# A four-layer transformer stack on one core: layer 3's experts put ahead of its shared products for the first half of the tokens, and the last spreads and gathers paced by landings and memsets

## The chip, the core and the metric

The kernel runs on one core of a Trainium2 chip. Its engines work in parallel, each through its own list of instructions in order: TensorE (PE: matrix products and transposes; PEld is its weight load), VectorE (DVE), ScalarE (ACT), GpSimd (POOL) and SyncE (SP, which here only issues DMAs). POOL issues the DMAs whose rows are chosen by an index (DMA_INDIRECT in the profile). The metric is the device time of one execution in microseconds (us), lower is better. Three runs of the kernel before gave 1930.78, 1930.79 and 1932.56 us; the median is 1930.79 us.

## The reference

An activation x of 4 x 1024 tokens with 128 features passes through four layers; each is `x = layernorm(x + mix(x))`, then `x = layernorm(x + ffn(x))`. Only layer 3 and one list of layer 1 are touched here. Layer 3, cut to what matters:

```
# mix: gated Toeplitz unit; t = position, mixing runs over the batch index
xr = x / (rms(x) + 1e-8)
u, v = silu(xr @ u_w.T + u_b), silu(xr @ v_w.T + v_b)          # 256 features each
x = layernorm(x + (u * toeplitz(v)) @ o_w.T + o_b + x)
# ffn: 32 experts, 4 of them for each token, and one shared product of width 512
p = softmax(x @ router_w.T + router_bias)
top, idx = top_k(p, 4);  top = top / sum(top)
routed = sum_i top[i] * ( silu(x @ gate[idx[i]].T) * (x @ up[idx[i]].T) ) @ down[idx[i]].T
shared = ( silu(x @ sgate.T) * (x @ sup.T) ) @ sdown.T
x = layernorm(x + routed + shared)
```

Layer 1's ffn has the same form with 16 experts, 4 for each token. All is float32.

## The kernel before

**Tokens and parts.** x stays in SBUF as 32 tiles of 128 tokens. Layer 3 treats them in three parts: `a` is the first half (16 tiles), `b` and `c` are a quarter each (8 tiles). Layer 1's second half is the part `r` (16 tiles).

**One part's way through a routed ffn.** `l3_attn` mixes, `l3_route` picks experts and computes for each token and choice a row in a list sorted by expert (`positions`, which writes `posl3b` and the like). `spread` (line 1373 on) then writes the tokens into that list in DRAM, one indirect DMA for each tile and choice: 64 for `a` or `r`, 32 for `b` or `c`; each carries 128 rows of 512 bytes. `small_experts` (lists `l3ra`, `l3rb`, `l3rc` in, `l3ya`, `l3yb`, `l3yc` out) reads the list in groups of four tiles (`xg`), multiplies by the experts' weights on PE (`gu`, `tp`, `yp`) and writes the results back to DRAM by SP; there are 20 groups for `a` and 12 for `b` and for `c`. Further groups that only an uneven routing needs stand under a condition at the end (`rest_of`, line 1414), which each engine evaluates for itself; the name `made l3a` is noted there. `collect` (line 1441) gathers each token's four results, one indirect DMA each into a buffer `yt`, and DVE adds them with their weights into x (line 1452). `finish` norms and writes out. `l3_shared` makes the shared products (`pg`, `pu`, `hs`, `py`); for `a` it adds straight into x, for `b` and `c` into a buffer that is added later (`held`).

**What sets the order.** The program is emitted by Python generators. Each step that a generator yields has a cost in planned microseconds. `mix(main, side, pace, drain)` emits a step of `main` and then steps of `side` until their costs, times `pace`, are used up; a larger pace uses a side step's cost up faster. `abreast` emits the generator that is behind next. `when` holds a chain until a name has been noted. Each engine then works in the order that came out. `indirect` also forces the indirect DMAs to stay on POOL's queue in the order of emission.

**Pacing.** Under `spaced(gen, 1, 2, 1.45)` every indirect DMA waits, on POOL, until the one two places ahead of it has landed (`before`, line 1345), and the planner counts 1.45 us for it in place of 1.26. In the kernel before this holds for `r`'s spread and gathers in layer 1, for all of layer 2 but its last gathers, and for `a`'s spread in layer 3. The spreads of `b` and `c` and all gathers of layer 3 go without.

**The last stretch.** After layer 2's last experts (`l2_experts(n2)`), `on` holds what runs beside PE's main work: the last gathers of layer 2, mixing and routing of `b`, its spread, mixing and routing of `c`, the 64 gathers of `a` with the spread of `c` somewhere between, and the gathers of `b`. The main work is, in this order: shared products of `a`, experts of `a`, shared products of `b`, experts of `b`, shared products of `c`, experts of `c`. At last `close` gathers the 32 results of each choice and tile of `c`, norms and writes out.

Of the kernel before, what the change touches and what calls it, by code (L numbers as in the profile page):

```python
# [20 lines left out]
P = 128  # L21
# [21 lines left out]
E3, F3, K3 = 32, 128, 4  # L43
# [31 lines left out]
class Kernel:  # L75
    def __init__(self, ctx, tc, ins, out, cols, consts, rows):
        self.tc, self.nc, self.ins, self.out = tc, tc.nc, ins, out
        self.count = itertools.count()
        nc = self.nc
        self.const = self.pool(ctx, "const")  # L80
        self.small = self.pool(ctx, "small", 3)
        self.routes = self.pool(ctx, "routes")
        self.side = self.pool(ctx, "side", 2, space=PSUM)
        dram = self.pool(ctx, "dram", space=DRAM)

        self.cols_t = self.load(self.const, ins["cols"])
        self.cst_t = self.load(self.const, ins["consts"])
        self.x = self.tile(self.const, [P, NT, D], "x")
        self.xT = self.tile(self.const, [P, NT * P], "xT")
        nrow = ins["rows"].shape[1]  # L90
        self.rows_t = self.tile(self.const, [P, nrow], "rows")
        nc.gpsimd.dma_start(out=self.rows_t, in_=ins["rows"].to_broadcast([P, nrow]))
        self.col = {k: self.cols_t[:, a:b] for k, (a, b) in cols.items()}
        self.cst = {k: self.cst_t[:, a:b] for k, (a, b) in consts.items()}
        self.row = {k: self.rows_t[:, a:b] for k, (a, b) in rows.items()}
        self.ident = self.cst["ident"]
        self.eps = self.tile(self.const, [P, 1], "eps")
        nc.vector.memset(self.eps, LN_EPS)
        self.halfpi = self.tile(self.const, [P, 1], "halfpi")
        nc.vector.memset(self.halfpi, math.pi / 2)  # L100
        self.ones = self.tile(self.const, [P, E3], "ones")
        nc.vector.memset(self.ones, 1.0)
        self.rnd = self.tile(self.const, [P, 1], "rnd")
        nc.vector.memset(self.rnd, RND)
        self.drop = self.tile(self.const, [P, 1], "drop")
        nc.vector.memset(self.drop, -RND)
        self.zero = self.tile(self.const, [P, D], "zero")
        nc.gpsimd.memset(self.zero, 0.0)
        self.flag = self.tile(self.const, [1, 1], "flag", I32)
        self.hm = self.tile(self.const, [P, 4], "hmg")  # L110

        self.first, self.rest = Part("a", 0, 2), (Part("b", 2, 1), Part("c", 3, 1))
        self.parts = (self.first, *self.rest)
        self.by_rows = (
            Part("a", 0, 2, range(B), 0), Part("m", 2, 2, (0, 1), NT // 2), Part("n", 2, 2, (2, 3), 3 * NT // 4)
        )

        self.rows_done = 0

        self.listed = set()  # L120

        self.traced, self.latest = nc.cur_bb.bb.instructions, {}
        self.now = self.moved_by = 0.0
        self.moved = []
        self.landing = []
        self.spacing = None

        self.lists, self.route = {}, {}
        self.both = (self.first, Part("r", 2, 2))
        for lay, ne, k in (("l1", E1, K1), ("l2", E2, K2), ("l3", E3, K3)):  # L130
            for pt in {"l1": self.both, "l2": self.by_rows, "l3": self.parts}[lay]:
                tl = -(-((pt.nt * P * k + (P - 1) * ne) // P) // 4) * 4
                self.lists[lay, pt.name] = (
                    self.tile(dram, [tl * P, D], f"{lay}r{pt.name}"), self.tile(dram, [tl * P, D], f"{lay}y{pt.name}"), tl
                )
        self.wall2 = self.tile(dram, [P, E2 * 3 * F2], "wall2")
        self.xsave = self.tile(dram, [P, NT, D], "xsave")

        self.ksave = self.tile(dram, [P, B, BLK], "ksave")
        self.vsave = self.tile(dram, [P, B, 4, (NH + 1) * VW], "vsave")  # L140
# [769 lines left out]
    def l2_attn(self, hf):  # L910
# [6 lines left out]
        with ExitStack() as low, ExitStack() as ctx:  # L917
# [114 lines left out]

            last = 4 * hf + 3
            d0, d1, d3 = (last - 3, 512), (last - 2, 384), (last, 128)
            full = [(j, 512) for j in range(4 * hf)]
            alone = lambda m: [[(m, *p) for p in ps] for ps in ([d0], [d1, d3])]
# [336 lines left out]
    def spread(self, lay, part, k):  # L1373

        pos, _, _, done, _ = self.route[lay + part.name]
        rows = self.lists[lay, part.name][0]
        for t in range(part.nt):
            for i in range(k):
                ins = self.indirect(
                    apart=done,  # L1380
                    out=rows, out_offset=bass.IndirectOffsetOnAxis(ap=pos[:, t, i : i + 1], axis=0),
                    in_=self.x[:, part.order[t], :], in_offset=None,
                )
                done.append(ins)
            yield (self.step * k,)
        self.listed.add(lay + part.name)

# [501 lines left out]
    def at_once(self, gen):  # L1889

        for _ in gen:
            yield (0.0,)

    def served(self, gen, *others):

        others = list(others)
        while True:
            while others and others[0][0]():
                yield from others.pop(0)[1]
            got = next(gen, None)  # L1900
            if got is None and not others:
                return
            yield got or (1.0,)
# [35 lines left out]
        yield from self.l2_route(part)  # L1939
        yield from self.spread("l2", part, K2)  # L1940

    def last(self, part, yp):
        yield from self.collect("l3", part, K3, yp)
        yield from self.finish(part)

    def close(self, part, yp):
# [10 lines left out]
    def all(self):  # L1957
        a, rest = self.first, self.rest
        b, c = rest
        r = self.both[1]  # L1960
        a2, m2, n2 = self.by_rows
        with ExitStack() as ctx:
            lgp = self.pool(ctx, "l2lg")
            self.l2_lg = self.tile(lgp, [P, NT, E2], "lg")
            with ExitStack() as early:
# [14 lines left out]
                with ExitStack() as c2:  # L1980
                    wall = self.l1_wall(c2)
                    yp = self.pool(c2, "l1ya", 5, right=True)
# [3 lines left out]
            with ExitStack() as c2:  # L1986
# [3 lines left out]
                yp = self.pool(c2, "l1yr", 5, right=True)  # L1990
                self.run(self.mix(self.chain(self.l1_experts(r, wall), self.l1_shared(r)), self.chain(loads, self.spaced(self.routed(a2), 1, 2, 1.45))))
                self.run(self.mix(self.l2_experts(a2, wall2), self.spaced(self.l1_close(r, yp), 1, 2, 1.45)))
            listed = lambda name: lambda: name in self.listed
# [6 lines left out]
            with ExitStack() as c3:  # L2000
                with ExitStack() as c2:
                    wall = self.l2_wall(c2)
                    self.press(on, listed("l2m"))
                    self.run(self.mix(self.l2_experts(m2, wall), on, drain=False))
                    self.press(on, lambda: {"l2n", "routed l3a"} <= self.listed)
                    sw, wall3 = self.l3_wall(c3, True)
                    on = self.chain(on, self.spaced(self.rows_in(m2), 1, 2, 1.45))
                    self.run(self.mix(self.l2_experts(n2, wall), on, drain=False))
                self.press(on, listed("l3a"))
                yp = self.pool(c3, "l3y", 8)  # L2010

                on = self.chain(
                    on, self.collect("l2", n2, K2, yp, which=(0, 1, 4, 5)),
                    self.abreast(
                        self.chain(self.l3_attn(b), self.mark("mixed l3b"), self.l3_route(b)),
                        self.collect("l2", n2, K2, yp, which=(2, 3, 6, 7)),
                    ),
                    self.abreast(
                        self.chain(
                            self.spread("l3", b, K3), self.when(listed("made l3a")), self.last(a, yp),  # L2020
                        ),
                        self.chain(
                            self.l3_attn(c), self.mark("mixed l3c"), self.l3_route(c),
                            self.at_once(self.spread("l3", c, K3)),
                        ),
                    ),
                    self.when(listed("made l3b")), self.last(b, yp),
                )
                self.run(self.mix(self.chain(self.l3_shared(a, sw), self.l3_experts(a, wall3)), on, 0.45, False))
                hold = self.pool(c3, "l3hold", 2)  # L2030
                for p in (b, c):
                    self.press(on, listed("mixed l3" + p.name))
                    sh = self.tile(hold, [P, QT, D], "sh")
                    self.run(self.mix(self.l3_shared(p, sw, sh), on, 0.75, False))
                    self.press(on, listed("l3" + p.name))
                    self.press(on, listed("mixed l3c"))
                    ahead = self.chain(self.held(p, sh), on) if p is c else self.held(p, sh)
                    self.run(self.mix(self.l3_experts(p, wall3, ahead), on, 0.75, False))
                self.run(self.close(c, yp))
        bad = self.nc.values_load(self.flag[0:1, 0:1], min_val=0, max_val=1)  # L2040
        with self.tc.If(bad > 0):  # L2041
            with ExitStack() as ctx:
# [9 lines left out]
                for p in self.parts:  # L2052
                    self.run(self.onward(p))
                    with ExitStack() as c2:
                        sw, wall = self.l3_wall(c2)
# [167 lines left out]
```

## Time and profile before

| what | value |
|---|---|
| median of three runs | 1930.79 us |
| the profiled execution, its own time | 1937.33 us |
| its span, first to last instruction | 1935.5 us |
| mean granted TensorE clock | 0.896 of full |
| busy in the span: PE / DVE / ACT / POOL | 1541.5 / 1199.2 / 900.6 / 690.3 us |
| layer 3's experts of `a`, their gathers start on POOL | 1712.8 us into the span |
| last matmul of `c`'s experts ends | 1865.6 us |
| `c`'s 32 gathers start | 1877.6 us |
| last of them is issued | 1920.3 us |

Durations below come from the profiled execution, whose own time is 6.5 us (0.34%) above the median of the runs. A row of the timeline gives start, duration, engine, source line, operation, tile written and read, and in brackets the idle time of the engine before it and what ended that idle time ("issue" is time for which the profile shows no wait). The share of a whole engine says little here: what counts is which engine has work without a gap in the last 400 us.

### The profile page before, as it was taken

To read this page: it belongs to the slowest core of one execution; us is meant where nothing else is said; L and a number is where in the kernel's file an instruction comes from. 1 tells how busy PE (TensorE), PEld (TensorE's weight loads), DVE (VectorE), ACT (ScalarE), POOL (GpSimd) and SP (SyncE) were. 2 spreads that over 40 slices of the span, in tenths; PEclk is the share of its full clock that TensorE was granted. 3 is DMA by queue.
4 is the path that set the end of the run, shared out by engine and by line. 5 is a ranking of instruction groups with operands and counts; after the bars stand their busy time and mean duration, and the time that the engine had idled before them with its cause. 6 is when DMAs were issued, how large, how long until landed. Compare 5 with 4: busy or idle time off the path is not lost. (4 is left out here: it accounts for less than half of the span.)

```text
span 1935.5 us, 27095 instructions
## 1 busy us (share of the span) xinstructions
PE 1541.5 (80%) x9025; PEld 920.8 (48%) x9025; DVE 1199.2 (62%) x3491; ACT 900.6 (47%) x1349; POOL 690.3 (36%) x670
## 2 busy tenths in 40 slices
PE   7885677597847887989977878798798998999850
PEld 3332433385423345856632232333355757768650
DVE  8998698465766664635564565546442446866383
ACT  5876265243324554423336756564532236644330
POOL 2000148604630660265443000030536430567775
PEclk9897688798978998999988988898988999989985
DMA  9990002244430113632241000000452213425452
GB/s 297 288 288 10 1 17 86 87 126 133 159 129 18 60 63 129 183 96 73 78 137 32 1 1 1 2 23 1 159 213 83 66 28 93 141 68 167 122 147 61
DMA packets 215530, 187.10 MB, mean 97 GB/s; under 512 B 16528, under 2 KB 194064, under 8 KB 214864
## 3 DMA queue, kind: packets, MB, share of 16 engines
q1 hardware_dynamic: 194672, 142.29, 23.6%
q0 software_dynamic: 20704, 42.86, 7.3%
q8 instruction: 84, 1.38, 0.3%
q14 instruction: 70, 0.57, 0.1%
HBM read 88.49 MB, written 96.60 MB: 96 GB/s over the span
## 5 line engine op out<-in xcount | busy, mean ns | idle before, releaser
L1081 ACT ACTIVATE pr<-sc 128x1024 f32<-128x1024 f32 x288 | 279.4, 1021 | 175.2 <-PE sc L161 174.8
L161 PE MATMUL sc<-qm,kT 32*128 32x512 f32 (+3 forms) x1536 | 197.7, 559 | 16.7 <-ACT pr L1081 16.7
L161 PE MATMUL s<-pr,va 128*32 128x512 f32 (+3 forms) x1536 | 167.5, 532 | 19.0 <-DVE x L1019 10.2
L161 PE MATMUL gu<-ld,xgT 128*128 x640 | 165.1, 400 | 10.2 <-DVE hg L1812 5.9
L1087 DVE TENSOR_TENSOR pr<-pr,ld 128x512 f32<-128x512 f32 (+1 forms) x160 | 91.7, 581 | 105.6 <-ACT pr L1081 105.4
L161 PE MATMUL gu<-wall,xgT 128*128 x304 | 148.2, 612 | 2.0 <-ACT xgT L171 2.0
L161 PEld LDWEIGHTS sc<-qm,kT 32*128 32x128 f32 x1536 | 83.7, 194 | 112.4 <-issue 61.1
L161 PEld LDWEIGHTS gu<-ld,xgT 128*128 128x128 f32 x640 | 119.5, 198 | 34.7 <-DVE hg L1812 6.1
L1812 DVE TENSOR_TENSOR hg<-sg,gu 128x256 f32<-128x256 f32 x160 | 66.0, 417 | 92.0 <-ACT sg L1811 91.6
L173 DVE COPY hT<-tp 128x512 f32<-128x512 f32 x118 | 80.9, 686 | 66.2 <-PE tp L169 66.2
L1567 ACT ACTIVATE sg<-gu 128x512 f32<-128x512 f32 x76 | 45.4, 597 | 144.7 <-PE gu L161 143.6
L1811 ACT ACTIVATE sg<-gu 128x256 f32<-128x256 f32 x160 | 61.3, 385 | 107.7 <-PE gu L161 79.8
L171 ACT COPY xgT<-tp 128x512 f32<-128x512 f32 x99 | 58.0, 586 | 99.9 <-PE tp L169 99.8
L1327 POOL DMA_INDIRECT l1ra<-x,posl1a x64 | 79.8, 1246 | 61.3 <-DVE peq L1321 42.0
L1327 POOL DMA_INDIRECT l1rr<-x,posl1r x64 | 65.4, 1022 | 100.9 <-DVE posl1r L1302 70.8
L169 PEld LDWEIGHTS tp<-ld,hg 128*128 128x128 f32 x624 | 77.4, 141 | 49.0 <-issue 32.5
L1569 DVE TENSOR_TENSOR hg<-sg,gu 128x512 f32<-128x512 f32 x76 | 51.8, 682 | 78.9 <-ACT sg L1567 78.8
L1327 POOL DMA_INDIRECT l2rm<-x,posl2m x16 | 15.7, 983 | 236.8 <-DVE peq L1320 230.1
L169 PE MATMUL tp<-ld,hg 128*128 128x128 f32 x624 | 96.4, 275 | 3.7 <-DVE hg L1812 2.0
L1327 POOL DMA_INDIRECT l3ra<-x,posl3a x64 | 63.7, 996 | 93.3 <-DVE usedl3a L1315 51.0
L161 PEld LDWEIGHTS s<-pr,va 128*32 128x32 f32 x1536 | 37.1, 113 | 122.6 <-issue 78.4
L161 PE MATMUL yp<-ld,hT 128*128 x640 | 86.1, 276 | 2.3 <-DVE mv L197 1.5
(447 smaller groups left out, 3439.1 us busy)
## 6 DMA issues: line engine op xcount, KB each, us to landing
wall<-wall SPq DMA_DIRECT2D x16, 768.0 KB, 7.8
l3ra<-zero SPq DMA_DIRECT2D x1, 6144.0 KB, 25.5
ld<-in_l_w SPq DMA_DIRECT2D x2, 3072.0 KB, 10.6
wall<-we SPq DMA_DIRECT2D x24, 256.0 KB, 2.1
ld<-in_l_w SPq DMA_DIRECT2D x1, 6144.0 KB, 20.6
l1ra<-zero SPq DMA_DIRECT2D x1, 5120.0 KB, 19.6
l1rr<-zero SPq DMA_DIRECT2D x1, 5120.0 KB, 23.1
xg<-l3ra SPq DMA_DIRECT2D x20, 256.0 KB, 2.9
```

The costliest lines, as they stand in the source:

```text
L161: return self.nc.tensor.matmul(out, lhsT, rhs, start=start, stop=stop)
L169: nc.tensor.transpose(pt[:, k * P : (k + 1) * P], s, self.ident)
L171: nc.scalar.copy(dst, pt[:, : n * P])
L173: nc.vector.tensor_copy(dst, pt[:, : n * P])
L1081: nc.scalar.activation(pr, sc[h], AF.Exp)
L1087: nc.vector.tensor_tensor(d, d, cst["tril"].unsqueeze(1).unsqueeze(1).to_broadcast([P, 2, n, P]), ALU.mult)
L1327: ins = self.nc.gpsimd.indirect_dma_start(**kw)
L1567: nc.scalar.activation(sg, gu[:, 0, :], AF.Silu)
L1569: nc.vector.tensor_tensor(h, sg, gu[:, 1, :], ALU.mult)
L1811: nc.scalar.activation(sg, pg[:, :, 0, :], AF.Silu)
L1812: nc.vector.tensor_tensor(h[:, 2 * c : 2 * c + 2, :], sg, pg[:, :, 1, :], ALU.mult)
```

## The change

Four edits, three of them in the last stretch.

1. Main work: the experts of `a` are emitted first and the shared products of `a` after them, in two `mix` calls. `a`'s gathers may so be emitted after its experts; `finish` of `a` waits for the new name `shared l3a`.
2. The spreads of `b` and `c` and the gathers of `a` and of `b` go under `spaced(..., 1, 2, 1.45)`. The gathers of `c` (`close`) and layer 2's last gathers stay as they were.
3. In `spread`, for the lists `l1r`, `l3b` and `l3c`, each indirect DMA is followed on POOL by a memset of a new tile `idle` (128 x 384 bytes) that nothing reads, and the next indirect DMA is queued behind it: 64 + 32 + 32 memsets.
4. The mixing and routing of `b` count 0.6 of their cost in the planner, so that they are emitted sooner beside the experts of `a`.

```diff
+        self.idle = self.tile(self.const, [P, 384], "idle", mybir.dt.uint8)
...
                     in_=self.x[:, part.order[t], :], in_offset=None,
                 )
                 done.append(ins)
+                if lay + part.name in ("l1r", "l3b", "l3c") and self.spacing:
+                    stay = self.nc.gpsimd.memset(self.idle, 0)
+                    self.tc.add_manual_dep(
+                        stay.ins, ins.ins.name,
+                        mybir.DependencyInfo(mybir.DependencyClass.NoSync, mybir.DependencyReason.DATA),
+                        reason="queued behind",
+                    )
+                    self.moved.append(stay.ins.name)
             yield (self.step * k,)
...
+    def scaled(self, gen, by):
+
+        for got in gen:
+            yield (got[0] * by, *got[1:])
...
-    def last(self, part, yp):
+    def last(self, part, yp, ready=lambda: True):
         yield from self.collect("l3", part, K3, yp)
+        yield from self.when(ready)
         yield from self.finish(part)
...
                     self.abreast(
-                        self.chain(self.l3_attn(b), self.mark("mixed l3b"), self.l3_route(b)),
+                        self.scaled(self.chain(self.l3_attn(b), self.mark("mixed l3b"), self.l3_route(b)), 0.6),
                         self.collect("l2", n2, K2, yp, which=(2, 3, 6, 7)),
                     ),
                     self.abreast(
                         self.chain(
-                            self.spread("l3", b, K3), self.when(listed("made l3a")), self.last(a, yp),
+                            self.spaced(self.spread("l3", b, K3), 1, 2, 1.45), self.when(listed("made l3a")),
+                            self.spaced(self.last(a, yp, listed("shared l3a")), 1, 2, 1.45),
                         ),
                         self.chain(
                             self.l3_attn(c), self.mark("mixed l3c"), self.l3_route(c),
-                            self.at_once(self.spread("l3", c, K3)),
+                            self.at_once(self.spaced(self.spread("l3", c, K3), 1, 2, 1.45)),
                         ),
                     ),
-                    self.when(listed("made l3b")), self.last(b, yp),
+                    self.when(listed("made l3b")), self.spaced(self.last(b, yp), 1, 2, 1.45),
                 )
-                self.run(self.mix(self.chain(self.l3_shared(a, sw), self.l3_experts(a, wall3)), on, 0.45, False))
+                self.run(self.mix(self.l3_experts(a, wall3), on, 0.45, False))
+                self.run(self.mix(self.chain(self.l3_shared(a, sw), self.mark("shared l3a")), on, 0.45, False))
```

In the built program the engines' lists differ from before only where these edits say: POOL has the 64 memsets in layer 1, and from layer 3 on the lists of all engines are reordered. POOL's order in the last stretch is: spread of `b` (30 of its 32 ahead of the condition after the experts of `a`), 32 gathers of `a`, spread of `c`, 32 gathers of `a`, 32 of `b`, 32 of `c`; apart from the memsets and the place of that condition it is the order of before.

## The prediction

> **What bounds the kernel now.** I read the end first, then back. The table by stretch, cut at PE's stages, is the first view (columns: stretch, its length, busy time of PE, PEld, DVE, ACT, POOL, TensorE clock, DMA share, GB/s):
>
> ```profile
> span 1935.5 us, 27095 instructions
> ...
> 1549.60:1708.00 158.40, 144.62 (x813) 110.29 (x813) 107.37 (x345) 83.08 (x157) 50.15 (x48) 0.99 0.30 90
> 1708.00:1743.00 35.00, 32.06 (x127) 20.13 (x125) 20.10 (x81) 15.74 (x25) 23.18 (x24) 0.80 0.20 52
> 1743.00:1793.00 50.00, 45.43 (x290) 40.55 (x288) 30.94 (x76) 23.59 (x49) 38.10 (x40) 0.97 0.57 168
> 1815.70:1866.00 50.30, 45.44 (x289) 40.53 (x288) 27.49 (x70) 23.62 (x49) 36.96 (x40) 0.97 0.63 166
> 1866.00:1921.50 55.50, 0.00 (x0) 0.00 (x0) 35.28 (x158) 3.35 (x8) 42.05 (x41) 0.54 0.35 92
> ```
>
> Up to 1866 PE is the busiest, over 90% of each stretch. After 1866 it has nothing: 70 us pass in which POOL issues gathers. So the second view is POOL's timeline, its turning points:
>
> ```profile
> 1657.54 1.36 POOL L1327 DMA_INDIRECT l3rb<-x,posl3b  x1 [85.27 <-ACT yg L1826]
> ...
> 1712.81 0.98 POOL L1327 DMA_INDIRECT yt<-l3ya,posl3a  x1 [10.81 <-SPq L1419]
> ...
> 1753.82 0.99 POOL L1327 DMA_INDIRECT l3rc<-x,posl3c  x1 [0.30 <-issue]
> ...
> 1794.90 0.99 POOL L1327 DMA_INDIRECT yt<-l3ya,posl3a  x1 [0.30 <-issue]
> ...
> 1836.44 0.94 POOL L1327 DMA_INDIRECT yt<-l3yb,posl3b  x1 [1.75 <-DVE x L1452]
> ...
> 1877.59 3.44 POOL L1327 DMA_INDIRECT yt<-l3yc,posl3c  x1 [1.28 <-DVE x L1452]
> ...
> 1920.27 0.94 POOL L1327 DMA_INDIRECT yt<-l3yc,posl3c  x1 [0.31 <-issue]
> ```
>
> From 1712.8 on POOL never rests: 32 + 32 + 32 + 32 indirect DMAs to 1876.3, one each 1.28 us (0.95 busy and 0.30 between two), then `c`'s 32. Results of `c` were there about 4 us after PE's last matmul (1865.6), so at 1869.6; their gathers began at 1877.6. POOL, not PE, ends last, by 8 us. From the first gather of `c` to the end of the span it takes 57.9 us.
>
> What a paced DMA costs is read where pacing is already in force. Third view, groups by operation (columns: count, busy us, mean ns, idle us before them and its causes), and the timeline of one quiet stretch:
>
> ```profile
> L1327 POOL DMA_INDIRECT l1rr<-x,posl1r x64 | 65.4, 1022 | 100.9 <-DVE posl1r L1302 70.8 <-DMA l1rr<-x,posl1r 23.8 <-issue 6.4
> L1327 POOL DMA_INDIRECT yt<-l1yr,posl1r x64 | 61.3, 957 | 57.4 <-DMA yt<-l1yr,posl1r 26.9 <-DVE x L1452 19.3 <-issue 6.3
> L344 POOL MEMSET keep<- 128x1024 f32 x1 | 1.0, 955 | 0.0
> L108 POOL MEMSET zero<- 128x128 f32 x1 | 0.2, 232 | 0.0
> L345 POOL MEMSET keep<- 128x4 f32 x1 | 0.1, 105 | 0.1
> ```
>
> ```profile
> 1520.34 0.94 POOL L1327 DMA_INDIRECT yt<-l2ym,posl2m  x1 [0.61 <-DMA yt<-l2ym,posl2m]
> 1521.59 0.94 POOL L1327 DMA_INDIRECT yt<-l2ym,posl2m  x1 [0.30 <-DMA yt<-l2ym,posl2m]
> 1523.14 0.94 POOL L1327 DMA_INDIRECT yt<-l2ym,posl2m  x1 [0.62 <-DMA yt<-l2ym,posl2m]
> 1524.39 0.95 POOL L1327 DMA_INDIRECT yt<-l2ym,posl2m  x1 [0.31 <-DMA yt<-l2ym,posl2m]
> ```
>
> The causes in brackets say that POOL stood until an earlier DMA had landed.
>
> **The change part by part.**
>
> *Order of the experts of `a`.* It gives `a`'s results earlier. It doesn't give POOL's queue an earlier start by as much, since the spread of `b` stands ahead of `a`'s gathers there; so I ask when that spread can begin. It needs `posl3b`. In the new order of PE and DVE `posl3b` falls between the groups 15 and 16 of the experts of `a`; attention of `b` begins at group 5. One group costs PE 3.55 us (the ups of `b`'s experts follow each other at that interval from 1758.6 to 1786.9). PE's part of mixing and routing `b` is 12.5 us (8 + 32 + 16 + 16 + 4 small matmuls: 3.8 + 3.9 + 2 + 2 + 1). Before, ten groups with such work beside them took 51.3 us (1605.3 to 1656.6) for 44.5 us of PE work, a factor of 1.15. Now: 5 us from 1549.6 to the first product (the experts must load `xg` first, as at 1743.1, where the first `gu` came 4.8 us later; the shared products needed no load, so this gap is new), 5 bare groups 17.7, then (39 + 12.5) x 1.15 = 59. `posl3b`, and the spread of `b`, at 1549.6 + 5 + 17.7 + 59 = 1631.5, against 1657.5: 26 us sooner. The experts of `a` end near 1660, their results are down at 1665, and POOL isn't done with the spread by then (below), so that they don't decide.
>
> *PE's own end.* The work is the same. It gains where PE idled and its clock fell to 0.80 (1704 to 1724, some 12 us over what the same matmuls take at full clock: mixing of `c` now lies beside 43 us of shared products of `a`), and loses the 5 us. I put the start of `b`'s experts at 1736 in place of 1743, the end of `c`'s at 1859, their results at 1863. DVE's adds of `a`'s gathers stand in DVE's order behind the shared products of `a` and in the experts of `b` and `c`; each gather has landed 10 us or more before its add, so that DVE doesn't stop PE. `b`'s list is complete at 1690, `c`'s at 1790, both ahead of their experts (1736, 1807).
>
> *Waits for landings.* 64 + 32 gathers and 32 + 32 scatters now wait. Nothing on POOL but the next indirect DMAs is queued behind a wait, yet these are what the end waits for. Nearest rows: paced gathers in layer 1 cost (61.3 + 26.9 + 6.3) / 64 = 1.48 us plus what hides in DVE's waits (19.3 us for buffers that come back late; a part would be landing time), and between 895 and 946, beside experts, 1.68; the quiet stretch above gives 2.80 us for two, 1.40. The last stretch moves more (DMA share 0.57 to 0.63, against 0.28 in layer 1). Bounds: 1.25 (no wait at all) and 1.70. I take 1.55.
> The Trainium skill, "DMA: Bandwidth & Descriptors", section "Anatomy of one DMA — SWDGE (gpsimd) path", has a fixed 2.0 us and bytes / 436 GB/s for such a DMA. One here has 64 KB, an estimate of 2.15 us; two places on at 1.25 us each leaves 2.5 us, so by the page the wait costs nothing, and 96 gathers take 120 us. The rows say 149. The traced waits decide: in the quiet rows above every second gather stood 0.3 us longer than the usual 0.30. The same section says that a semaphore wait is held by the issuing sequencer, not by the DMA engines; that speaks against the change, and the trace shows it as POOL's idle time.
>
> *Memsets.* No row has one of bytes. The three rows above fit 0.105 us and 0.83 ns for each element of a partition. 384 elements so cost 0.42 us; if four bytes went as one element, 0.18. Either adds to the 1.26 us between scatters unless it hides in their 0.30; it also covers landing time: paced scatters without it cost (65.4 + 23.8 + 6.4) / 64 = 1.49 on average. Bounds: 1.45 (all hidden, or wider spacing making landings quicker) and 1.90. I take 1.26 + 0.42 and a little left of the stalls: 1.70.
> In layer 1 the 64 with memsets take 109 us from 629, and land at 741. `xg` of `l1rr` is issued at 745.5, when PE is done with attention's transposes, and PE's own order holds its first use to 756. Cost nothing; cover up to a pace of 1.8.
>
> *Sum on POOL.* From the start of `b`'s spread: 64 scatters x 1.70 = 109 and 96 gathers x 1.55 = 149, so `c`'s gathers could begin at 1631.5 + 258 + 1 = 1890. Before: 1877.6. PE's 1863 is covered. Late by 12. In the last 57.9 us two of the first three gathers of `c` took 3.44 and 2.06 us, beside the write-out of `a`; that will be over by 1890, 3 us less. The net is +9 us on the profiled execution's 1937.3; it stands 6.5 us above the median, and I carry the difference over: 1930.8 + 9 = 1940.
>
> **The rivals.**
> 1. *The head start outweighs the waits: PE is the bound (faster).* POOL's start is 26 us sooner and each paced DMA dearer, so there is a point: with the start at 1631.5 all is even at (1876.3 + 3 - 1631.5) / 160 = 1.55 us for each of the 160. If gathers go at 1.40 as in the quiet rows and scatters at 1.55, the chain is 99 + 134 = 233, `c`'s gathers begin at 1866, 11 us sooner, and with the 3 us of the tail the time is 1917. For: the quiet rows. Against: DMA share twice as high.
> 2. *Near balance.* 1.48 and 1.62, or the spread starting 8 us sooner: 1930.
> 3. *Waits much longer.* Scatters at 1.9 and gathers at 1.65, as in the busy part of layer 1: 280 us, `c`'s gathers at 1912.5, and DVE begins to wait for `a`'s second half inside `c`'s experts: 1962 and over.
> 4. *The change not doing what it says:* the built order has the memsets between the scatters and experts first; what could be void is the wait, if landings always came in time. That is the page's case in its pure form and ends in rival 1's bound by PE.
>
> **How the numbers follow.** My forecast (POOL's chain longer than its head start, 1935 to 1955) 0.60; rival 1 with 4, 0.25; rival 2, 0.10; rival 3, 0.05. A measurement of this kernel can tell 0.2%, 3.9 us, from no change. Faster 0.25, same 0.10, slower 0.65. The range for 8 in 10 is 1919 to 1955: it leaves out the better half of rival 1 and the worst of the forecast and rival 3. My forecast's own range is 1935 to 1955, from 0.07 us on 96 gathers, 0.1 us on 64 scatters and 7 us on the start.
>
> **What would show it.** Right: spread of `b` starting near 1630, `a`'s gathers near 1686 with POOL waiting for landings of `yt` and not for `made l3a`; 1.7 us from scatter to scatter; `c`'s gathers starting 25 us after PE's last matmul, directly behind `b`'s. Wrong: POOL idle ahead of `c`'s gathers until results of `c` land (rival 1); memsets of 0.2 us; PE waiting on `l3rb` or `l3rc`, or DVE on `yt<-l3ya` within the experts (rival 3); a later start of `l1r`'s experts.

## The result, and the profile after

The changed kernel takes 1966.14 us (median of 4 runs, 1963.22 to 1974.65) against 1931.67 (4 runs, 1930.78 to 1935.29): a ratio of 1.0178, with a 95% interval from 1.0155 to 1.020. It is 34.5 us slower. Forecast were 9 us and a range up to 1955. The direction was right, and the size was not. The profiled execution of after took 1963.22 us, 2.9 below its median; that of before took 1937.33, 5.7 above its own. So the two spans differ by 25.9 us only, and the profiles alone can't account for all of the 34.5; the experiments have to. Ratios here and below leave out executions that lie over 1.5% above the fastest of the same kernel, so a ratio can differ from that of the two medians.

The table by stretch of after, cut at PE's stages (columns as before: length, busy time of PE, PEld, DVE, ACT, POOL, TensorE clock, DMA share, GB/s):

```profile
span 1961.4 us, 27225 instructions
...
1548.90:1600.00 51.10, 43.50 (x229) 33.85 (x229) 30.02 (x88) 28.52 (x57) 15.16 (x16) 0.93 0.48 130
...
1700.00:1745.50 45.50, 44.70 (x223) 29.67 (x222) 32.87 (x113) 12.28 (x19) 31.35 (x36) 1.00 0.17 46
...
1818.60:1868.10 49.50, 45.21 (x288) 40.60 (x288) 27.95 (x72) 23.29 (x48) 26.32 (x28) 0.97 0.56 155
```

PE ends layer 3's experts at 1868.1 (before 1865.6). The shared products now run at the full clock (1.00 in 1700 to 1745; 0.80 before), but in the first stretch of the experts PE idles 7.6 us of 51.1. PE's last matmuls, of before and of after:

```profile
1863.24 2.38 PE L161 MATMUL yp<-ld,hT 128*128 x16
...
1865.91 2.15 PE L162 MATMUL yp<-ld,hT 128*128 x16
```

POOL's timeline, the same turning points as before:

```profile
1639.48 1.02 POOL L1328 DMA_INDIRECT l3rb<-x,posl3b  x1 [66.93 <-issue]
...
1693.60 0.99 POOL L1328 DMA_INDIRECT yt<-l3ya,posl3a  x1 [0.17 <-issue]
...
1739.65 0.99 POOL L1328 DMA_INDIRECT l3rc<-x,posl3c  x1 [1.08 <-ACT sg L764]
...
1796.92 0.99 POOL L1328 DMA_INDIRECT yt<-l3ya,posl3a  x1 [0.34 <-issue]
...
1853.55 0.94 POOL L1328 DMA_INDIRECT yt<-l3yb,posl3b  x1 [1.78 <-DVE x L1461]
...
1907.52 0.95 POOL L1328 DMA_INDIRECT yt<-l3yc,posl3c  x1 [0.30 <-issue]
...
1946.27 0.94 POOL L1328 DMA_INDIRECT yt<-l3yc,posl3c  x1 [0.30 <-issue]
```

The spread of `b` starts 18 us sooner than before, and yet `c`'s gathers start 30 us later, 39 us after PE's last matmul. Between the two lie 268.0 us in which POOL goes from one indirect DMA to the next. What each kind costs, from the groups by operation (count, busy us, mean ns, idle us before them and its causes), and from the list of DMA issues (the last column is the median us from issue to landing):

```profile
L1328 POOL DMA_INDIRECT yt<-l3ya,posl3a x64 | 61.0, 952 | 39.4 <-DMA yt<-l3ya,posl3a 29.4 <-issue 3.6 <-DVE x L1461 3.5
L1387 POOL MEMSET idle<- 128x384 uint8 x128 | 56.2, 439 | 0.1
L1328 POOL DMA_INDIRECT yt<-l3yb,posl3b x32 | 32.7, 1022 | 22.8 <-DMA yt<-l3yb,posl3b 12.4 <-DVE x L1461 5.2 <-issue 2.4
...
L1328 POOL DMA_INDIRECT l3rc<-x,posl3c x32 | 31.2, 975 | 12.9 <-issue 5.1 <-DMA l3rc<-x,posl3c 4.8 <-ACT sg L1820 1.4
```

```profile
yt<-l3ya,posl3a POOLq DMA_INDIRECT x64, 2.6
l3rb<-x,posl3b POOLq DMA_INDIRECT x32, 2.2
...
yt<-l3yb,posl3b POOLq DMA_INDIRECT x32, 2.5
```

The gathers stand 41.8 us for landings of their own kind (29.4 + 12.4). A landing takes 2.2 to 2.6 us in these rows (the prediction's estimate was 2.15), about as long as two undisturbed pitches (2 x 1.25 us). So a wait two places on is reached just before the landing, and most gathers pay a part. The memset of 439 ns (estimated at 0.42) stands behind each scatter.

### The profile page after: what moved, and what is told of

It reads as the page before. It is cut to its first block, busy times and chain, and to the rows that moved or that the text cites. A ratio compares the mean times of both kernels' runs of the same rounds, so it can differ in the third digit from the quotient of the medians.

```text
span 1961.4 us, 27225 instructions
## 1 busy us (share of the span) xinstructions
PE 1540.2 (79%) x9025; PEld 924.1 (47%) x9025; DVE 1203.3 (61%) x3491; ACT 897.7 (46%) x1348; POOL 741.2 (38%) x798
## 5 line engine op out<-in xcount | busy, mean ns | idle before, releaser
L170 PE MATMUL tp<-ld,xg 128*128 128x128 f32 x396 | 66.3, 294 | 27.8 <-DMA xg<-l2rm 5.8
```

Of the source, the lines that this page charges most:

```text
L170: nc.tensor.transpose(pt[:, k * P : (k + 1) * P], s, self.ident)
```

## The experiments

Ratios are to before on the same chip. On the chips of e1 to e4 and of f1 to f4 before itself took 1931.6 and 1932.2 us; on those of the other runs it took 2264 (e5 to e8), 2232 (g1 to g4) and 2234 (h1, h2). So the results stand in two groups, and no time of one is set against a time of the other.

**The changed kernel again** (`f4_after`, unchanged).

> The changed kernel itself, beside the others on the same chip. Where before takes about 1931: 1966, as measured. Where before takes 2264: theory (there unpaced indirect DMAs leave engines standing for tens of us, and pacing them frees these) the memsets of layer 1 bring 56 us and the paced last stretch 74 us as each did alone, so 2130 to 2150, faster than before by 5%; rival (both remedy the same stall) 2190, as either alone.

Measured, beside a before of 1932.19: 1966.33 us, 1.0177 (1.0157 to 1.0197). The result stands a second time.

**Order only** (`e1_order_only`): the four `spaced` of the last stretch taken out, with them the memsets of layer 3. Those of layer 1 stay.

```diff
-  self.spaced(self.spread("l3", b, K3), 1, 2, 1.45), self.when(listed("made l3a")),
-  self.spaced(self.last(a, yp, listed("shared l3a")), 1, 2, 1.45),
+  self.spread("l3", b, K3), self.when(listed("made l3a")),
+  self.last(a, yp, listed("shared l3a")),
...
-  self.at_once(self.spaced(self.spread("l3", c, K3), 1, 2, 1.45)),
+  self.at_once(self.spread("l3", c, K3)),
...
-  self.when(listed("made l3b")), self.spaced(self.last(b, yp), 1, 2, 1.45),
+  self.when(listed("made l3b")), self.last(b, yp),
```

> The new order of layer 3's first half with its scaling of 0.6 and the memsets in layer 1, but the last two spreads and the gathers of a and b unpaced, without memsets. Theory (pacing is what costs): 160 indirect DMAs at 1.26 us are 202 us from about 1639, POOL is through with b's gathers near 1845 and waits for c's results, which are down some 4 us after PE's last matmul at 1868; c's gathers start near 1873, end near 1928 of the span, 33 us sooner than the changed kernel: about 1930. Rival A (the reordering itself costs, by PE or by waits between stages): 1950 or more. Rival B (unpaced landings collide and the results come later): PE ends after 1880, 1940 or more.

Measured 1932.08 us, 0.9999 (0.9987 to 1.0011): 34 us less than the changed kernel, no difference from before. POOL's timeline of this run, and PE's last matmuls:

```profile
1643.59 1.02 POOL L1328 DMA_INDIRECT l3rb<-x,posl3b  x1 [67.15 <-issue]
...
1810.35 0.94 POOL L1328 DMA_INDIRECT yt<-l3yb,posl3b  x1 [0.56 <-DVE x L1461]
...
1880.03 1.10 POOL L1328 DMA_INDIRECT yt<-l3yc,posl3c  x1 [18.73 <-DVE x L1461]
...
1872.31 2.17 PE L162 MATMUL yp<-ld,hT 128*128 x16
```

Unpaced, POOL is through with the rest at 1861.3, and then stands 18.7 us. What it waits for comes with the end of PE's work: PE's last matmul ends at 1874.5, the last of `c`'s results is on its way at 1875.5, and DVE, which has `b`'s adds in its order behind `c`'s experts, gives buffers back from 1874.2 on. PE is the bound, as in rival 1 of the prediction. So the pacing of the last stretch costs the 34 us, less than its 50 us on POOL's chain (268.0 against 1861.3 - 1643.6 = 217.7), because POOL has 19 us to spare. (Without `spaced` the planner also counts 1.26 us for such a DMA again, so the order of the other engines moves a little: PE ends at 1874.5 here, at 1868.1 in the changed kernel.)

**One half of the pacing each** (`e2_spreads_paced`: `spaced` taken from the gathers of `a` and `b`; `e3_gathers_paced`: taken from the two spreads, whose memsets go with it).

> The changed kernel with the gathers of a and b unpaced; the two spreads keep their waits and memsets. Theory (costs add up along POOL's chain): 64 scatters 111 us as measured, 96 gathers at 1.26 us 121 us, from 1639 to 1871; c's gathers at 1873 from POOL and PE alike, about 1930. Rival (landing time is only pushed from one place to the next, so that unpaced gathers run into buffers that aren't back): b's gathers end after 1885, 1945 or more.

> The changed kernel with the two spreads unpaced and without memsets; the gathers of a and b keep their waits. Theory: 64 scatters at 1.26 us 81 us, 96 gathers 157 us as measured, 238 us from 1639 to 1877; c's gathers near 1878, some 30 us sooner than the changed kernel: about 1936. Rival (spreads run closer make the gathers' landings slower): gathers at 1.8 us, about 1950.

Measured 1940.25 us, 1.0045 (1.0022 to 1.0069) for e2, and 1947.16, 1.0082 (1.005 to 1.0114) for e3. Over the run without pacing that is 8 and 15 us, together 23, and both together cost 34: each alone uses up the same spare time of POOL first. In e3 `b`'s gathers end at 1889.3 and `c`'s begin at 1889.6, 14 us after PE's end (1875.2), so that POOL has become the bound:

```profile
1888.31 1.00 POOL L1328 DMA_INDIRECT yt<-l3yb,posl3b  x1 [0.55 <-DMA yt<-l3yb,posl3b]
1889.62 0.99 POOL L1328 DMA_INDIRECT yt<-l3yc,posl3c  x1 [0.30 <-issue]
```

In e2 POOL is through at 1873.5, and `c`'s gathers begin at 1879.1, after 5.6 us of waiting for DVE's adds; its profiled execution, 4 us under its median, does not show where the 8 us are. Both came out 10 us above the expectation. In e3 POOL's chain took 246.1 us where I had put 238, and began 4.5 us later than I had put it; for e2 the reason stays open.

**No memsets in layer 3** (`e4_no_memset`), waits kept:

```diff
-  if lay + part.name in ("l1r", "l3b", "l3c") and self.spacing:
+  if lay + part.name in ("l1r",) and self.spacing:
...
```

> The changed kernel without the 64 memsets in the last two spreads; all waits for landings stay. Theory (each memset adds nearly its 0.44 us, landings are mostly there by then): scatters at 1.45 us, 16 to 18 us off POOL's chain: about 1949. Rival (the wait for the landing takes the memset's place): scatters stay at 1.7 us, 1963 to 1967, no difference.

Measured 1960.93 us, 1.0141 (1.0111 to 1.0171): some 5 us less than the changed kernel, which is not clear of noise, as the two intervals overlap. The scatters of `b` take 50.0 us instead of 54.1, those of `c` 53.2 instead of 57.3 (1.56 and 1.66 us each): 28 us of memsets removed, 8 us gained, of which the gathers behind them give 4 back (POOL's chain is 263.9 us instead of 268.0). Most of what a memset takes, the wait for the landing takes in its absence; the rival was nearly right.

**Waits four places on** (`e8_four_back`, and the same kernel as `f3_four_back`): `1, 4, 1.45` for `1, 2, 1.45` in the four places, no memsets in layer 3, those of layer 1 kept.

> The changed kernel with waits four places on and no memsets in layer 3, a second time. Where before takes about 1931: theory (a landing takes under 4 pitches of 1.25 us, so that such a wait is void) 1931 to 1936, as without pacing; rival (landings come in only every 1.5 us) 1950 or more. Where before takes 2264: 2198 again, of which the memsets in layer 1 bring most.

Measured, where before takes 1932.19: 1940.82 us, 1.0035 (1.0014 to 1.0055), 25 us less than the changed kernel. The groups of that run:

```profile
L1328 POOL DMA_INDIRECT yt<-l3ya,posl3a x64 | 61.2, 956 | 19.5 <-issue 18.3 <-DVE hg L1821 0.3 <-DMA yt<-l3ya,posl3a 0.3
L1328 POOL DMA_INDIRECT l3rc<-x,posl3c x32 | 31.1, 971 | 9.8 <-issue 7.4 <-DMA l3rc<-x,posl3c 2.1 <-ACT xgT L172 0.3
L1328 POOL DMA_INDIRECT yt<-l3yb,posl3b x32 | 30.8, 961 | 37.9 <-DVE x L1461 29.4 <-issue 7.3 <-DVE hg L1821 0.9
```

Waits for landings fell from 29.4 us to 0.3 on `a`'s gathers and vanished on `b`'s: two places on is inside the landing time, four is outside. What is left over order only, some 7 us by the two ratios (1.0035 and 0.9999), is not on landings: `b`'s gathers stand 29.4 us for DVE's adds, which free their buffers. A step of 1.45 us instead of 1.26 in the order's planning puts these adds later in DVE's order; that this is the cause was not tried by itself.

**Layer 1's memsets alone** (`e5_l1_memset`, and the same kernel as `f1_l1_memset`): before, and behind each scatter of `l1r`

```diff
+  if lay + part.name in ("l1r",) and self.spacing:
+      stay = self.nc.gpsimd.memset(self.idle, 0)
...
```

> The kernel before with the memset behind each of layer 1's 64 scatters of the remaining tokens and nothing else, a second time. On a chip where before takes about 1931, the theory (their landing isn't waited for) says 1931 to 1933; the rival (they push layer 1's experts back, as first xg at 751.2 instead of 745.5 in the changed kernel) 1935 to 1938. On a chip where before takes 2264, as in the last call: 2208 again, since engines stand there for tens of us in waits that no instruction of the trace ends ('issue', 'remote'), beside unpaced indirect DMAs.

Measured, where before takes 1932.19: 1940.12 us, 1.0042 (1.0026 to 1.0057). What the prediction had put down at nothing costs 8 us, more than either side of the expectation had. Groups of DVE and the loads behind layer 1's attention, first of before, then of this run (groups by operation from 629 to 745; the tile `l1rr`, with the first and last start in us):

```profile
L1087 DVE TENSOR_TENSOR pr<-pr,ld 128x512 f32<-128x512 f32 x36 | 24.7, 687 | 14.2 <-ACT pr L1081 14.1
...
L964 DVE TENSOR_SCALAR qm<-qT,hmg 128x512 f32<-128x512 f32 x8 | 3.5, 498 | 0.1
L213 DVE TENSOR_SCALAR x<-x,mv,rstd 128x128 f32<-128x128 f32 x12 | 3.4, 374 | 0.1
...
L1327 POOL DMA_INDIRECT l1rr<-x,posl1r x64: 953/960/1581, 629.0 to 723.7; - x64
L1392 SPq DMA_DIRECT2D xg<-l1rr x18: 359/363/1357, 745.5 to 815.7; - x18
```

```profile
L1088 DVE TENSOR_TENSOR pr<-pr,ld 128x512 f32<-128x512 f32 x34 | 23.4, 689 | 11.9 <-ACT pr L1082 11.8
L965 DVE TENSOR_SCALAR qm<-qT,hmg 128x512 f32<-128x512 f32 x8 | 4.9, 676 | 0.1
L214 DVE TENSOR_SCALAR x<-x,mv,rstd 128x128 f32<-128x128 f32 x12 | 4.2, 530 | 0.1
...
L1328 POOL DMA_INDIRECT l1rr<-x,posl1r x64: 964/964/1431, 631.3 to 736.8; - x64
L1401 SPq DMA_DIRECT2D xg<-l1rr x18: 359/363/1107, 752.1 to 822.5; - x18
```

Beside the memsets the tensor-scalar operations are longer, from 498 to 676 ns and from 374 to 530; the tensor-tensor products `pr` of the same length are not (687, 689). Every other profile from a chip on which before takes 1931 agrees: in the same window it is 609 to 744 and 529 to 530 ns with these memsets (seven profiles), 497 and 349 without them (f2). The Trainium skill, "SBUF — State Buffer", section "Who interferes with whom", has a mechanism for this: DVE in a two-port mode, which tensor_scalar can enter and tensor_tensor cannot, and any GpSimd instruction share one pair of ports, and whichever comes second stands for the whole of the first. The rows agree with that, though none shows the mode. Layer 1's experts start later: from the first scatter to the first `xg` it takes 116.5 us in before and 114.6 in f2, and with the memsets 120.8 here and 121.7 to 127.1 in the seven others. It is not the scatters' later landing. The first `xg` is issued when PE's attention ends, with the transposes of `o`, in all of these profiles; their rows in before and here:

```profile
744.71 0.73 PE L169 MATMUL s<-ld,o 128*128 128x128 f32 x4 [0.28 <-DVE o L1002]
...
751.30 0.73 PE L170 MATMUL s<-ld,o 128*128 128x128 f32 x4 [0.28 <-DVE o L1003]
```

By then more than 14 us had passed since the start of the last scatter (736.8), and PE's wait for these rows hardly changed (3.6 us in before, 3.8 here). So attention itself is slower beside the memsets, and DVE's longer rows are the one cause that the profiles show. That they make up all of the 8 us is not shown: the two tensor-scalar groups above are busy only 2.2 us longer.

With e1 this gives an estimate of the order's worth. Order with these memsets is level with before (0.9999), the memsets alone are at 1.0042: by the difference of the two ratios the order brings 8 us, with some 4 us of uncertainty. The profiles say less: from layer 3's start to the end it takes 385.9 us in before and 387.5 in f1, and 383.8 in e1, which is 2 to 4 us. There POOL's lag behind PE shrinks from 12.0 us (1865.6 to 1877.6) to 5.5 (1874.5 to 1880.0), while PE's stretch from layer 3's start grows from 316.0 to 321.7.

**The scaling alone** (`e7_old_order_scaled`, and the same kernel as `f2_old_order_scaled`): before, with

```diff
-  self.chain(self.l3_attn(b), self.mark("mixed l3b"), self.l3_route(b)),
+  self.scaled(self.chain(self.l3_attn(b), self.mark("mixed l3b"), self.l3_route(b)), 0.6),
```

> Before with the scaling by 0.6 of attention and routing of b alone, a second time. Where before takes about 1931: theory (POOL ends late by 8 us, an earlier spread of b gives them back) 1922 to 1927; rival (POOL waits for a's results instead) 1930 to 1933. Where before takes 2264: 2283 again.

Measured, where before takes 1932.19: 1935.7 us, 1.002 (1.0007 to 1.0033). The spread of `b` starts at 1639.7 as in the changed kernel, but in the order that comes out `c`'s spread stands behind it, and POOL is idle 25 us ahead of that. `a`'s gathers begin at 1750.5, and `c`'s at 1876.3 against 1877.6:

```profile
1710.13 0.95 POOL L1327 DMA_INDIRECT l3rc<-x,posl3c  x1 [25.35 <-ACT yg L1826]
...
1750.51 0.99 POOL L1327 DMA_INDIRECT yt<-l3ya,posl3a  x1 [0.30 <-issue]
```

The rival was right that nothing is gained (the time is 3 us above its range): without the experts first, the earlier spread has no use.

**The chips on which before takes 2232 to 2264.** Here some of the same kernels stand the other way round. The expectations of these runs, each under its name, come first, then the edits and the results in one table. `e5` (layer 1's memsets alone):

> The kernel before with one addition: a memset of 128x384 bytes behind each of layer 1's 64 scatters of the remaining tokens; layer 3 as before. Theory from the prediction (nothing waits for these scatters until PE is done with attention): 1931 to 1933, no difference. Rival (the scatters' last landing, some 11 us later, or PE's attention beside them is delayed, as the changed kernel's trace has it: first xg of layer 1's remaining tokens issued at 751.2 instead of 745.5): 4 to 6 us slower, 1936 to 1938.

`e6` (old order, paced last stretch):

> The kernel before with its old order (shared products first, no scaling), and in the last stretch the waits two places on for the spreads of b and c and the gathers of a and b, with the memsets behind the scatters of these spreads; layer 1 as before. Theory (the pacing makes POOL's chain 268 us long whatever the order, and the order moves only its start): spread b at 1657.5, c's gathers at 1926, 48 us later than before and 18 later than in the changed kernel: about 1980. Rival (beside other work the paced DMAs are cheaper): below 1966.

`e7` (the scaling alone):

> The kernel before with the scaling by 0.6 of attention and routing of b alone: shared products of a first, nothing paced in the last stretch, no memsets. Theory (before is POOL-bound at the end by 8 us only, PE's end is next): spread b starts 15 to 25 us sooner, c's gathers follow c's results at about 1870, 1922 to 1927. Rival (a's results aren't there when b's spread is done, and POOL waits for them): POOL's chain starts again at the same 1712, no difference, 1930 to 1933.

`e8` (waits four places on):

> The changed kernel with the waits of the last stretch four places on instead of two, and without memsets in layer 3 (those of layer 1 stay). Theory (the landing takes some 3 us, so that a wait two places on at a 1.25 us pitch stands and one four places on does not): POOL's chain shrinks to about 1.3 us each, PE bounds, 1932 to 1936 as with no pacing at all. Rival (the DMA engines deliver an indirect DMA only every 1.5 us or more here, and any wait stands for it): scatters and gathers stay at 1.5 to 1.7 us, 1950 or more.

`g1` (the order alone):

> The new order of layer 3's first half with the scaling, and nothing else: no memset anywhere, nothing newly paced. Theory (the order gains about 8 us, the memsets of layer 1 had eaten them in the run of the order with these): 1922 to 1926, faster than before by 0.4%. Rival (the gain of the order is only the noise between two calls): 1930 to 1934.

`g2` (the changed kernel without layer 1's memsets):

> The changed kernel without the memsets in layer 1; layer 3 as changed. Theory (the delay of layer 1 is carried to the end, since nothing between has slack): 1956 to 1960. Rival (the last stretch is bound by POOL and takes up the delay): 1965 to 1967.

`g3` (as e6):

> The old order (shared products of a first, no scaling) with the paced spreads and gathers and their memsets in layer 3, none in layer 1, a second time. Where before takes about 1931: theory (POOL's chain of 268 us starts at 1657 instead of 1639, and it bounds): c's gathers at 1926, 1975 to 1982. Rival (the chain is shorter where it starts later, as PE's and SP's transfers collide less with it): 1950 to 1962. Where before takes 2264: 2190 again.

`g4` (layer 1's memsets behind its scatters):

> The kernel before with 64 memsets of 128x384 bytes put in one block behind the last of layer 1's 64 scatters, not between them. The scatters land as before. Theory A (a memset makes DVE's operations stand, on which PE waits in attention): DVE rows longer between 725 and 755, 3 to 8 us slower, 1935 to 1940. Theory B (it was the scatters' later landing): no difference, 1931 to 1933.

`h1` (as g1):

> The new order of layer 3's first half with the scaling, and nothing else, a second time. Where before takes about 1931: theory (the order gains 8 us) 1922 to 1926; rival (no gain) 1930 to 1934. Where before takes 2232 to 2264: no difference, as in the last call.

`h2` (as e6):

> The old order with the paced last stretch and its memsets, none in layer 1, a third time. Where before takes about 1931: theory (POOL's paced chain of 268 us starts at 1657 instead of 1639, and it bounds) 1975 to 1982; rival (the chain is shorter where it starts later) 1950 to 1962. Where before takes 2232 to 2264: 2155 to 2190, as in the last two calls.

The edits that are new: `e6`, `g3` and `h2` are before with `spaced(..., 1, 2, 1.45)` around the two spreads and the gathers of `a` and `b`, and memsets for `("l3b", "l3c")`; `g1` and `h1` are e1 with no memsets at all (`in ()`); `g2` is the changed kernel with memsets for `("l3b", "l3c")` only; `g4` has the 64 memsets of layer 1 in one loop behind the last scatter:

```diff
+  if lay + part.name == "l1r":
+      for _ in range(part.nt * k):
+          stay = self.nc.gpsimd.memset(self.idle, 0)
...
```

| kernel | before there | time | ratio (95%) |
|---|---|---|---|
| e5: memsets between layer 1's scatters | 2264 | 2208.5 | 0.9754 (0.9709 to 0.9798) |
| g4: the same memsets behind them | 2232 | 2241.6 | 1.010 (1.003 to 1.017) |
| e6, g3, h2: old order, paced last stretch | 2264, 2232, 2234 | 2190.5, 2155.2, 2168.4 | 0.9678, 0.9738, 0.9725 (0.9655 to 0.9796) |
| e7: scaling alone | 2264 | 2282.8 | 1.0078 (1.0038 to 1.0118) |
| e8: e5 and the order, waits four places on | 2264 | 2198.5 | 0.9718 (0.9677 to 0.9759) |
| g1: order alone | 2232 | 2233.4 | 1.0038 (0.9988 to 1.0089) |
| g2: changed kernel without layer 1's memsets | 2232 | 2141.5 | 0.9658 (0.9585 to 0.9731) |

(`h1`, the order alone a second time, had a median of 2246.95 beside 2234.03, and no ratio was formed. For the three runs in one row the interval is that of the last.) The view of waits of g1, and then of g2, both on one chip (engine, line, what it waited for: us in total, times, longest):

```profile
ACT pr L1082 <- remote: 82.2, 7, 51.5
DVE hs L765 <- remote: 58.1, 3, 48.3
ACT sg L764 <- remote: 53.4, 5, 28.6
```

```profile
ACT pr L1082 <- remote: 62.6, 11, 29.9
ACT sg L764 <- remote: 28.9, 3, 13.3
DVE x L1020 <- remote: 25.9, 1, 25.9
```

"Remote" is a release by nothing that the trace knows. No such wait stands in any of the ten profiles from chips on which before takes 1931. Two of them, on ACT in e7, the second among the longest (start, length, operation, in brackets the idle time before it), while POOL issued unpaced scatters and then gathers one after another:

```profile
1974.35 0.60 ACT L763 ACTIVATE sg<-pg 128x512 f32<-128x512 f32 x1 [13.19 <-remote]
2035.28 0.59 ACT L1769 COPY sh<-py 128x512 f32<-128x512 f32 x1 [60.33 <-remote]
```

So there, engines stand for tens of us beside rows of indirect DMAs with nothing between them, and room between the DMAs helps: memsets between the scatters do (e5), the same memsets behind them don't (g4, though on another of these chips), waits two places on with memsets do (e6), and waits four places on, with the order, add nothing to layer 1's memsets that can be told from e5 (e8). What the engines wait for, and why on these chips and not on the others, stays open. The changed kernel as a whole did not run on such a chip, nor the order alone on a chip of the other kind; g2, which is the change without its memsets in layer 1, is 3.4% faster there. The order alone gained nothing in g1 and h1, where theory had hoped for 8 us in the first.

This leaves untested that layer 1's share is additive within the changed kernel (g2), that the order alone gains where before takes 1931 (g1, h1), and that POOL's chain in the old order ends at 1926 there (e6, g3, h2). The same holds for g4's question, landing or DVE; the rows of f1 rule out the landing, and leave DVE likely.

## Why the prediction was right in direction and wrong in size

The direction, and the reason given for it, held: POOL's paced chain became longer than its head start, PE's end stayed covered, `c`'s gathers followed directly on `b`'s, `a`'s gathers waited for landings of `yt` and not for `made l3a`. Rival 1 failed by its own point of balance, 1.55 us for each DMA: measured are 268.0 / 160 = 1.675. Rival 4 (void waits, because landings always come in time) failed too; f3 shows that it holds four places on, not two. Rival 3, with a chance of 0.05, had the measured time (1962 and over) and nearly the price of a gather (1.65, measured 1.63), but not its way: scatters took 1.74 us and not 1.9, DVE did not wait for `a`'s second half inside `c`'s experts, and 8 of the 34.5 us lie in layer 1, where no rival had any. One sign that the prediction had named as wrong was seen, a later start of `l1r`'s experts (751.2 against 745.5). The sum failed at three terms, each worth some 8 us: layer 1's memsets (put at nothing), PE's work for the mixing and routing of `b`, and the price of a gather. Step by step:

1. *Layer 1's memsets: predicted 0, measured 8* (f1, 1.0042). The step that failed asked only who waits for the scatters' rows, and found them covered up to a pace of 1.8 us. That much was right. It did not ask whom the memset itself disturbs: PE's attention beside it ended later, and DVE's rows are longer.
2. *Start of `b`'s spread: predicted 1631.5, measured 1639.5* (second profile 1642.2). The gap for `xg` was right (5 predicted, 4.67 on PE), and so was the end near the 16th group. Wrong was "PE's part of mixing and routing `b` is 12.5 us": in after it is 20.45. PE's rows for it from 1584.10 to 1638.70 (length, busy time), the groups of its first products in that stretch, and the same products in before between 1593.5 and 1605.3:

```profile
1584.10:1638.70 54.60, 20.45 (x85) 0.97 0.30 84
L162 PE MATMUL s<-xq,ld 128*128 128x512 f32 x16 | 9.2, 706 | 1.4 <-ACT xq L172 0.8 <-ACT v L1646 0.6
...
L161 PE MATMUL s<-xq,ld 128*128 128x512 f32 x8 | 3.8, 606 | 0.0
L169 PE MATMUL s<-ld,sq 128*128 128x128 f32 x8 | 1.2, 272 | 0.0
```

There are 16 products `s<-xq` (9.2 us) where the prediction's list has 8 (3.8 us), and the other groups are together 2.5 us longer than its list. The stretch of before from which it took its factor of 1.15 begins at 1605.3, behind the first 8 of them. With 20.45 in its own sum the spread starts at 1549.6 + 5 + 17.7 + (39 + 20.45) x 1.15 = 1640.7; in after the factor is 54.5 / (8 x 3.55 + 20.45) = 1.12. The "5 bare groups" were wrong too, as eight stand ahead of attention's first product (1584.15), but this alone makes the sum 2 us shorter and not longer, since three groups fewer then follow.

3. *64 scatters: predicted 109, measured 54.1 + 57.3 = 111.4.* The memset's size was right, and so, within 0.04 us, was the sum. e4 shows why it is no plain addition: 20 of the 28 us of memsets stand where a landing wait would.
4. *96 gathers: predicted 149 at 1.55, measured 46.1 + 56.6 + 54.0 = 156.7, 1.63 each.* The first 32, beside the shared products, took 1.44; the later 64, beside experts, 1.77 and 1.69, above the row of 1.68 from the busy part of layer 1 that I had averaged with quiet ones. Most of the gathers lie in the busy part, and should have been priced by it.
5. *Tail: predicted 54.9, measured 53.9.*
6. *PE: predicted to end 7 us sooner, measured 2.4 later.* The clock of the shared products rose as foreseen (0.80 to 1.00), but PE's busy time from layer 3's start to its end stayed at 289 us (289.2 and 288.8), so the gain put on that clock did not come. Beside the 4.67 us for `xg`, PE also idles 4.45 for a square root of ACT in the mixing of `c`:

```profile
1553.59 2.33 PE L170 MATMUL tp<-ld,xg 128*128 128x128 f32 x8 [4.67 <-DMA xg<-l3ra]
...
1641.35 3.06 PE L162 MATMUL gu<-ld,xgT 128*128 x8 [4.45 <-ACT rms L1666]
```

It cost nothing in this kernel, as POOL bounds; in e1 PE bounds, and the order could not bring what the prediction had hoped of PE.

From layer 3's start to the end, before takes 1935.5 - 1549.6 = 385.9 us and after 1961.4 - 1548.9 = 412.5: 26.6 longer, of which the prediction had 9; steps 2 to 5 give the difference (8.7 counted from layer 3's start, 2.4, 7.7, -1.0, together 17.8). With step 1's 7.9 us (1940.1 against 1932.2) the 26.6 come to 34.5, what was measured; that it fits to a tenth is luck, since each of the two is good to some us. The range was too narrow because layer 1's memsets stood in it with one value, nothing, and the start of `b`'s spread with an error of 7 us where a part of PE's work was missing.

## What to carry to other kernels

A wait put into a queue costs what is left of the awaited time when the queue gets there: where a landing takes two pitches, a wait two places on stands most of the time, and one four places on doesn't. A filler instruction on an idle engine is priced twice, by its own queue and by what it does to other engines; look at their rows beside it, even where nothing waits for it. Before a stretch of an old trace is used as a price, count that all of the work to be priced lies in it. And compare kernels only beside the same reference on the same chip: here the sign of one edit changed from chip to chip.

## What the runs showed of the hardware

A memset of 128x384 bytes on POOL takes 439 ns (as 384 elements would by the fit to the memsets of four-byte elements, so four bytes don't go as one), and behind it the next indirect DMA follows 0.17 us later instead of 0.30. Beside such memsets DVE's tensor-scalar operations of 128x512 took 676 ns instead of 498 (f1). On three chips of those that the runs fell on, the kernel before took 2232 to 2264 us instead of 1931. The profiles of other kernels there have waits of up to 73 us on ACT and DVE (the longest on DVE in e7) that no event of the trace ends. The change without layer 1's memsets took away 3.4% there (g2), and pacing the last stretch cost 1.8% on the other chips (after against e1).
